# Layer 0's last pair of panels: two of its four tiles get their expert scores from TensorE, after a transpose inside the lone last panel

## The chip, the cores and the metric

The kernel runs on one core of one Trainium2 chip. The metric is the device time in microseconds of one execution; the time before is the median of three runs. A profile is one further execution, recorded instruction by instruction. Engines are named as in the profile: PE is TensorE (PEld its weight loads), DVE is VectorE, ACT is ScalarE, POOL is GpSimd, SP is the engine that issues most DMAs.

## The reference

Two layers act on 3327 nodes of 256 features. Layer 0 is

```python
x = x + relu(adj @ (layernorm(x) @ W) + b)                      # graph part
h = layernorm(x)
scores = h @ Wg.T + bg                                          # 8 experts
top2, which = top_k(scores, 2); share = softmax(top2)
x = x + sum over the two experts e of share_e * (relu(h @ W1[e].T + b1[e]) @ W2[e].T + b2[e])
```

Layer 1 has the same shape: a graph part whose adjacency is filtered by tanh(adj * adj), and a mixture of eight experts (256 by 256, gelu, two of eight per token). Everything is float32. The change concerns only `scores` of layer 0, for 256 of the 3327 tokens.

## The kernel before

**Tiling.** Nodes are padded to 3328 = 26 tiles of 128. A panel is 256 nodes (two tiles); there are 13 panels, and each has two adjacency pieces of 1.7 MB in a ring of six buffers. `x` and the support `s` stay in SBUF.

**Layer 0's graph part** is `aggregate_first` (L482). It takes panels 0 and 1 side by side, then the pairs (2,3) to (10,11) through `pair` (L571), and then panel 12 alone, the lone last panel, through `rest` (L558). `rest` runs j over the 26 tiles of source nodes; each j is two matmuls into the two PSUM banks of the panel (L495). After step `behind_` it calls `finish` (L512), and where `hooks` has an entry for j it calls that function. For the last panel the call is

```python
        rest(NPAN - 1, 0, {CJ: layer0.turn_first}, LAST_BEHIND)     # L649: CJ = 13, LAST_BEHIND = 11
```

so `finish` runs after j = 11 and works on the pair (10,11), and after j = 13 the tokens of expert block 0 are transposed (`turn_first`, L1172).

**What `finish` does for a pair.** It lists the tokens of the pair before it (`listed`), multiplies the aggregated features by the weights (`weigh`, L506) with `add_relu` on DVE (L403, L404), and then runs the generator `route0` (L1508) to its end:

1. `normalized`: statistics on DVE (L337 to L354), and for four tiles the scaling on ACT (L360), tile by tile into two `xn` buffers of two tiles each.
2. `scores` (L656): for each tile and each of eight experts one DVE product with a row of `gate` that also sums it (L662, 128x256): 32 of them for four tiles.
3. `weights` (L720): bias, ranking, the two best, `rt_both` (L700), which tells the two experts of each token.

For the earlier pairs, `pair` spreads the three steps with `next(routing)`; the last pair gets all of them in the one call.

**Listing.** `list_tokens` (L759) counts places with small matmuls on PE (`pr`, L770 and L771: from `rt_both` and the running sums `cum`), and POOL scatters each token to the lists of its two experts (`xlist`, L793). PE takes its queue in order. The last pair is listed inside expert block 0: `layer0.step(None, between=finish_last)` (L1539) runs the first product of the block (L1226), then `finish` for the lone panel, which begins with listing the pair. After that stand the transposes of block 1's tokens (L1172) and the second product of block 0 (L1323). The lone panel's own routing runs on DVE during block 1, and `plan` (L947) needs its counts.

**PSUM.** Pool `psh` (two banks) serves `ps_o` of `weigh`, `ps_h` and the turned tokens `ptb`; pool `pst` (two banks) serves `pt`, `pg`, `pr` and `pc`.

**Scores by PE** exist already in layer 1: for its lone panel, `by_features` (L377) transposes two tiles through PE and ACT copies them out (L387, L388), and `scores_by_product` (L668) multiplies them by the router `f1_r_sb` (L672), with a copy by DVE (L681). The start of the kernel loads `f1_r_sb` and four other constants through POOL's queue (L1489).

Of the kernel before, what the change touches and what calls it, by code (L numbers as in the profile page):

```python
# [10 lines left out]
F32 = mybir.dt.float32  # L11
# [11 lines left out]
P = 128  # L23
NT = 26
NP = NT * P
D = 256
DC = D // P
E = 8
H = 1024
PW = 256  # L30
NPAN = NP // PW
NCHUNK = 2
CJ = NT // NCHUNK
# [44 lines left out]
BEHIND, LAST_BEHIND = 5, 11  # L78
# [49 lines left out]
def gnn_moe_two_layers(  # L128
# [26 lines left out]
    const = ctx.enter_context(tc.tile_pool(name="const", bufs=1))  # L155
    state = ctx.enter_context(tc.tile_pool(name="state", bufs=1))
    work = ctx.enter_context(tc.tile_pool(name="work", bufs=3))
# [131 lines left out]
    def follow(later, earlier):  # L289
        for o in earlier:  # L290
            tc.add_manual_dep(later.ins, o.ins.name, after, reason="same rows of DRAM")
# [27 lines left out]
    def load_gate(g):  # L319
        nc.gpsimd.dma_start(  # L320
            out=gate.rearrange("p e d -> p (e d)"),
            in_=g.rearrange("e d -> (e d)").unsqueeze(0).partition_broadcast(P),
        )
# [53 lines left out]
    def by_features(xn, n, name="xnT"):  # L377

        return turned_tiles([xn[:, g, 0, :] for g in range(n)], name)

    def turned_tiles(tiles, name):
        n = len(tiles)
        xnT = work.tile([P, DC, n * P], F32, name=name, bufs=2)
        pt = pst.tile([P, DC, n * P], F32, name="pt", tag="pt")
        for g in range(n):
            for c in range(DC):
                nc.tensor.transpose(pt[:, c, ts(g, P)], tiles[g][:, ts(c, P)], ident)  # L387
        nc.scalar.copy(xnT, pt)  # L388
        return xnT
# [92 lines left out]
    def aggregate_first(b_sb, w, w_sb, begin, count, route, listed, freed):  # L482
# [10 lines left out]
        def add(pan, j):  # L493
            for c in range(DC):
                nc.tensor.matmul(  # L495
                    sums[pan][c],
                    lhsT=s[:, j, ts(c, P)],
                    rhs=piece(pan, j // CJ)[:, j % CJ, :],
                    start=(j == 0),
                    stop=(j == NT - 1),  # L500
                )

        def weigh(pan, g, it):
            ps = psh.tile([P, D], F32, name="ps_o", tag="ph")
            for c in range(DC):
                nc.tensor.matmul(  # L506
                    ps, lhsT=g[:, c, ts(it, P)], rhs=w_sb[:, c, :], start=(c == 0),
                    stop=(c == DC - 1),
                )
            add_relu(x[:, pan * (PW // P) + it, :], ps, b_sb)  # L510

        def finish():  # L512
            if not waiting:
                return
            todo = list(waiting)
            waiting.clear()
            if todo[0][0] < NPAN - 1:
                listed()
            for pan, g in todo:
                for it in range(PW // P):  # L520
                    weigh(pan, g, it)
            if todo[0][0] == NPAN - 1:
                listed()
            for _ in route([pan for pan, _ in todo]):
                pass

        def finishing():
# [9 lines left out]
        def sums_of():  # L537
            return work.tile([P, DC, PW], F32, name="xnT", bufs=2)

        def copy(out, ps):  # L540
            copied.append(nc.scalar.copy(out, ps))

        def count_next():
            if counts:
                count(*counts.pop(0), copied)
# [12 lines left out]
        def rest(pan, first, hooks=(), behind_=BEHIND):  # L558
            hooks = dict(hooks)
            for j in range(first, NT):  # L560
                add(pan, j)
                if j == first + behind_:
                    finish()
                if j in hooks:
                    hooks[j]()
            g = sums_of()
            for c in range(DC):
                copy(g[:, c, :], sums[pan][c])
            waiting.append((pan, g))
# [76 lines left out]
        sums[NPAN - 1] = banks[0:2]  # L646
        for _ in range(NCHUNK):
            count_next()
        rest(NPAN - 1, 0, {CJ: layer0.turn_first}, LAST_BEHIND)  # L649
        return finish  # L650

    def rows_of(a, t0, n):
        return a[t0 * P : (t0 + n) * P, :].rearrange("(n p) d -> p n d", p=P)


    def scores(xns, n, all_n=None):  # L656
        sc = work.tile([P, all_n or n, E], F32, name="rt_sc", bufs=2)
        for g in range(n):
            xn = xns[g // 2][:, g % 2, 0, 0:D]
            for e in range(E):  # L660
                product = work.tile([P, D], F32, name="rt_product", bufs=1)
                nc.vector.scalar_tensor_tensor(  # L662
                    product, xn, 1.0, gate[:, e, :], ALU.mult, ALU.mult,
                    accum_out=sc[:, g, e : e + 1],
                )
        return sc

    def scores_by_product(xnT, n, w_sb, sc=None):  # L668
        pg = pst.tile([P, n, E], F32, name="pg", tag="pt")
        for g in range(n):  # L670
            for c in range(DC):
                nc.tensor.matmul(  # L672
                    pg[:, g, :],
                    lhsT=xnT[:, c, ts(g, P)],
                    rhs=w_sb[:, c, :],
                    start=(c == 0),
                    stop=(c == DC - 1),
                )
        if sc is None:
            sc = work.tile([P, n, E], F32, name="rt_sc", bufs=2)  # L680
        nc.vector.tensor_copy(sc, pg)  # L681
        return sc
# [37 lines left out]
    def weights(sc, n, bias=None, now=False):  # L720


        if bias is not None:
            nc.vector.tensor_tensor(sc, sc, bias.unsqueeze(1).to_broadcast([P, n, E]), ALU.add)
        sel, top, both = top_two(sc, n)
        d = work.tile([P, n], F32, name="rt_d", bufs=2)
        nc.vector.tensor_tensor(d, top[:, :, 1], top[:, :, 0], ALU.subtract)
        if now:
            nc.scalar.activation(d, d, AF.Exp)
            return sel, both, shares(d, n)  # L730
        return sel, both, d
# [9 lines left out]
    def normalized(t, n, on_scalar=False):  # L741

        stats = statistics(t, n)
        if not on_scalar:
            return [layernorm(t + at, 2, stats, at) for at in range(0, n, 2)]
        shift = shifted(*stats, n)
        xns = [work.tile([P, 2, K, RW], F32, name="xn") for _ in range(0, n, 2)]
        for g in range(n):
            scaled(xns[g // 2][:, g % 2, 0, 0:D], t + g, g, stats[1], shift)
        return xns  # L750
# [726 lines left out]

    g1_wg_sb = const.tile([P, DC, D], F32, name="g1_wg_sb")
    f1_r_sb = const.tile([P, DC, E], F32, name="f1_r_sb")
    f1_b1_sb = const.tile(list(f1_b1.shape), F32, name="f1_b1_sb")  # L1480
    g1_bp_sb = const.tile(list(g1_bp.shape), F32, name="g1_bp_sb")
    for t, w in [
        (gnn_b_sb, g0_b[0:1, :].partition_broadcast(P)),
        (g1_wg_sb, g1_wg.rearrange("(c p) n -> p c n", p=P)),
        (f1_r_sb, f1_rT.rearrange("(c p) n -> p c n", p=P)),
        (f1_b1_sb, f1_b1),
        (g1_bp_sb, g1_bp),
    ]:
        follow(nc.gpsimd.dma_start(out=t, in_=w), last_normalized)  # L1489

    def count(pan, k, copied):
# [8 lines left out]
    layer0 = experts(  # L1500
        xlist0, ys0, "0", FIXED[0], H, AF.Relu, f0_w1T, f0_b1, f0_w2T, f0_b2,
        nc.scalar.copy, BLOCKS0, seven=range(3, EARLY + LATE_PAIRS + FIXED[0] - 1),
    )

    def tiles_of(pans):
        return pans[0] * (PW // P), len(pans) * (PW // P)

    def route0(pans):  # L1508
        if pans[0] == 0:
            load_gate(gates[0])  # L1510
        t, n = tiles_of(pans)
        xns = normalized(t, n, on_scalar=n == 4)
        yield
        sc = scores(xns, n)
        yield
        routed.append((xns, *weights(sc, n, f0_bg_sb), t, n, xlist0, "0"))

# [15 lines left out]
    def begin(pan):  # L1533
        if pan in (1, 8):
            fill(xlist0 if pan == 1 else xlist1)

    finish_last = aggregate_first(gnn_b_sb, g0_w, proj_sb, begin, count, route0, listed0, freed0)

    layer0.step(None, between=finish_last)  # L1539
# [192 lines left out]
    with tc.If(first_usual > 0) as arms:  # L1732
# [29 lines left out]
        with tc.If(second_usual > 0) as inner:  # L1762
# [8 lines left out]
            while len(layer1.started) < layer1.always:  # L1771
# [6 lines left out]
                with behind(last_y):  # L1778
                    if asked and asked[0][2] + 1 < at <= layer1.always - FIXED[1]:
                        yt, tiles, _ = asked.pop(0)  # L1780
                        add_loaded(yt, *tiles)
                        added.append((tiles, at))
                if waiting and at > waiting[0][1] + (1 if k < FIRST_TILES // 2 else 2):
                    tiles, _, written = waiting.pop(0)
# [4 lines left out]
                if at in (EARLY + E, EARLY + 2 * E):  # L1789
                    tiles = range(0, FIRST_TILES, 2) if at == EARLY + E else range(FIRST_TILES, MORE_TILES, 2)  # L1790
# [185 lines left out]
```

## Time and profile before

| | us |
|---|---|
| median of 3 runs (1186.8 to 1188.58) | 1188.58 |
| the profiled execution | 1192.74 |
| its span, first to last instruction | 1191.0 |
| DVE busy | 867.1 |
| products for scores, L662, x400 records | 194.9 |
| two-bank matmuls of side-by-side and lone panels, L495, x312 records | 70.2 |

A row of the profile's groups reads: line, engine, operation, output<-inputs, shapes, count, then busy time and mean duration, then the idle time of the engine just before these instructions and what ended it. The mean granted TensorE clock of the execution is 0.989 of full speed. Of 40 equal slices of the span, here is the share of PE, of DVE and the granted clock, in tenths (9 is 90% or more); the lone last panel and the first expert blocks lie in slices 10 to 12 (about 268 to 357 us):

```
PE   8999999999899999999999999999999999999973
DVE  6698999988885555454545669289999998785454
PEclk9999999999999999999999999999999999999996
```

### The profile page before, as it was taken

The numbers are of one execution on the slowest core, as the hardware profiler recorded it, in microseconds if no ns is written. First come the engines' busy times: TensorE is split into PE (matmuls) and PEld (weight loads), VectorE is DVE, ScalarE is ACT, GpSimd is POOL, SyncE is SP. The second block draws the span as 40 slices with busy tenths as digits, with TensorE's granted clock in tenths as the row PEclk, the third lists the DMA queues.
The fourth block names the chain that finished last, engine by engine and source line by source line (L and its number), as shares of the span: only waits on it lengthen the run. The fifth ranks groups of instructions, "written<-read, shape, count | busy, mean of one in ns | idle before, by whom it ended". The sixth has DMA issues, their size and how long they took to land. (4 is left out here: it accounts for less than half of the span.)

```text
span 1191.0 us, 19704 instructions
## 1 busy us (share of the span) xinstructions
PE 1152.0 (97%) x6217; PEld 1005.4 (84%) x6217; DVE 867.1 (73%) x3001; ACT 557.0 (47%) x1051; POOL 290.5 (24%) x367
## 2 busy tenths in 40 slices
PE   8999999999899999999999999999999999999973
PEld 7888888888788888888888888888888888888852
DVE  6698999988885555454545669289999998785454
ACT  5599647540233333434333346985455562043321
POOL 2111332242331112111111010022232232265531
PEclk9999999999999999999999999999999999999996
DMA  9896738724376555757565955145354451479696
GB/s 349 180 265 260 241 127 239 257 88 152 125 260 224 195 186 187 270 182 258 199 219 168 386 208 201 65 183 180 144 204 166 161 200 55 134 229 273 202 288 207
DMA packets 123185, 241.68 MB, mean 203 GB/s; under 512 B 24480, under 2 KB 93120, under 8 KB 116160
## 3 DMA queue, kind: packets, MB, share of 16 engines
q1 hardware_dynamic: 108656, 205.59, 52.7%
q0 software_dynamic: 11136, 31.60, 7.2%
q10 hardware_dynamic: 3280, 3.15, 0.8%
q8 instruction: 51, 0.84, 0.3%
q14 instruction: 62, 0.51, 0.1%
HBM read 203.98 MB, written 36.33 MB: 202 GB/s over the span
## 5 line engine op out<-in xcount | busy, mean ns | idle before, releaser
L440 PE MATMUL ps_g<-s,ring 128*128 128x256 f32 x1352 | 294.2, 380 | 0.0
L440 PEld LDWEIGHTS ps_g<-s,ring 128*128 128x128 f32 x1352 | 256.0, 190 | 34.4
L1234 ACT ACTIVATE pad<-ps_h,ring 128x256 f32<-128x256 f32 (+1 forms) x282 | 128.9, 458 | 287.2 <-PE ps_h L1226 156.1
L1226 PE MATMUL ps_h<-pad,ring 128*128 128x256 f32 (+1 forms) x1184 | 254.4, 367 | 4.4 <-ACT pad L1176 4.1
L1226 PEld LDWEIGHTS ps_h<-pad,ring 128*128 128x128 f32 x1184 | 200.9, 190 | 46.7 <-ACT pad L1234 11.1
L662 DVE SCALAR_TENSOR_TENSOR rt_product<-xn,gate 128x256 f32<-128x256 f32 x400 | 194.9, 487 | 16.1 <-ACT xn L360 2.8
L793 POOL DMA_INDIRECT ys<-pad,index x114 | 115.7, 1015 | 363.8 <-DVE pad L1281 236.1
L793 POOL DMA_INDIRECT xlist<-xn,rt_idx x104 | 115.0, 1106 | 156.9 <-DVE ln_nw L347 60.9
L1495 ACT ACTIVATE sign<-ring,below 128x416 bf16<-128x416 f32 x208 | 133.4, 641 | 13.8 <-DMA ring<-in_adjT 7.8
L470 PE MATMUL ps_g<-ring,pad 128*128 128x256 f32 x520 | 115.1, 380 | 0.8 <-DMA ring<-in_adjT 0.8
L470 PEld LDWEIGHTS ps_g<-ring,pad 128*128 128x128 f32 x520 | 98.4, 190 | 14.4 <-DMA ring<-in_adjT 1.2
L1660 ACT ACTIVATE ring<-ring 128x3328 f32<-128x3328 f32 x22 | 65.4, 2979 | 87.3 <-DVE ring L1659 56.2
L1281 DVE SCALAR_TENSOR_TENSOR pad<-ps_y,ring,pad 128x128 f32<-128x128 f32 x176 | 59.3, 348 | 47.5 <-PE ps_y L1274 47.3
L470 PE MATMUL ps_g<-ring,s 128*128 128x256 f32 x390 | 89.6, 379 | 0.0
L470 PEld LDWEIGHTS ps_g<-ring,s 128*128 128x128 f32 x390 | 74.1, 190 | 10.1
L480 DVE TENSOR_TENSOR ring<-ring,ring 128x768 f32<-128x768 f32 (+1 forms) x80 | 79.7, 1014 | 0.0
L495 PE MATMUL ps_g<-ring,s 128*128 128x256 f32 x312 | 70.2, 386 | 4.4 <-ACT s L360 4.4
L495 PEld LDWEIGHTS ps_g<-ring,s 128*128 128x128 f32 x312 | 60.1, 194 | 13.5 <-ACT s L360 5.2
L1661 ACT ACTIVATE ring<-ring 128x3328 f32<-128x3328 f32 x22 | 65.4, 2979 | 0.6
L1265 DVE TENSOR_TENSOR xnT<-pad 128x512 f32<-128x512 f32 x22 | 15.2, 692 | 59.2 <-ACT pad L1234 59.2
L1323 PE MATMUL ps_y<-ring,pad 128*128 128x256 f32 x224 | 53.8, 386 | 0.0
L776 POOL COPY xn<-rt_w 128x4 f32<-128x4 f32 x26 | 4.8, 198 | 197.8 <-DVE rt_w L738 197.8
(240 smaller groups left out, 1584.3 us busy)
## 6 DMA issues: line engine op xcount, KB each, us to landing
ring<-in_adjT SPq DMA_DIRECT2D x50, 1664.0 KB, 8.2
ring<-in_f_w1T SPq DMA_DIRECT2D x30, 1024.0 KB, 5.7
ring<-in_f_w2T SPq DMA_DIRECT2D x30, 1024.0 KB, 8.0
ring<-xlist SPq DMA_DIRECT2D x52, 258.0 KB, 3.5
ring<-in_f_w SPq DMA_DIRECT2D x36, 256.0 KB, 3.8
ring<-ys SPq DMA_DIRECT2D x12, 512.0 KB, 4.2
ring<-in_f_b SPq DMA_DIRECT2D x34, 128.0 KB, 7.6
xlist<-h2T SPq DMA_DIRECT2D x16, 257.0 KB, 7.8
```

Of the source, the lines that this page charges most:

```text
L440: nc.tensor.matmul(ps[it], lhsT=chunks[k][:, c, ts(it, P)], rhs=s[:, j, :], start=(j == 0), stop=(j == NT - 1),)
L470: nc.tensor.matmul(ps, lhsT=b[:, c, :], rhs=a[:, c, :], start=(first and c == 0), stop=(c == CJ - 1), skip_group_check=not first,)
L480: nc.vector.tensor_tensor(out[:, part, :], out[:, part, :], other[:, part, :], ALU.add)
L495: nc.tensor.matmul(sums[pan][c], lhsT=s[:, j, ts(c, P)], rhs=piece(pan, j // CJ)[:, j % CJ, :], start=(j == 0), stop=(j == NT - 1),)
L662: nc.vector.scalar_tensor_tensor(product, xn, 1.0, gate[:, e, :], ALU.mult, ALU.mult, accum_out=sc[:, g, e : e + 1],)
L793: d = nc.gpsimd.indirect_dma_start(out=a[:, :], out_offset=bass.IndirectOffsetOnAxis(ap=index, axis=0), in_=rows_, in_offset=None,)
L1226: last_product[:] = [nc.tensor.matmul(ps, lhsT=w1[:, c, ts(hc, P)], rhs=xT[:, c, :], start=(c == 0), stop=(c == DC - 1),)]
L1234: nc.scalar.activation(hT[:, hc, :], ps, func, bias=bb1[:, hc : hc + 1])
L1281: last_y[:] = [nc.vector.scalar_tensor_tensor(part, ps, xb[:, g, WT : WT + 1], part, ALU.mult, ALU.add)]
L1495: nc.scalar.activation(sign, piece(pan, k)[:, :, ts(i, GROUP)], AF.Sign, bias=below, accum_out=positive[:, pan, i, k : k + 1],)
L1660: nc.scalar.activation(a, a, AF.Square)
L1661: nc.scalar.activation(a, a, AF.Tanh)
```

## The change

The routing of the last pair is cut in three. `finish` runs only its first part (statistics and scaling), two new hooks of `rest` run the others: after j = 20, tiles 0 and 1 of the pair are transposed by PE and copied out by ACT; after j = 25, the last one, tiles 2 and 3 are scored by DVE as before (16 products), tiles 0 and 1 by four matmuls on PE with the gate weights `f0_wg_sb`, and then come the ranking and the rest. `f0_wg_sb` is one more constant, loaded at the start through POOL's queue, between `f1_r_sb` and `f1_b1_sb`. `scores` takes a range of tiles in place of an unused parameter. In the changed program the listing of the last pair and the transposes of block 1's tokens stand one after the other on PE, where they were interleaved with the first matmuls of `ps_y`; on ACT the Exp of the last pair stands after the eight `ps_h` rows of block 0, and the Exp of the lone panel before the copy of block 2's turned tokens.

```diff
@@ aggregate_first: finish
             if todo[0][0] == NPAN - 1:
                 listed()
-            for _ in route([pan for pan, _ in todo]):
+            routing = route([pan for pan, _ in todo])
+            if len(todo) == 1:
+                for _ in routing:
+                    pass
+            else:
+                next(routing)
+                last_pair.append(routing)
+
+        last_pair = []
+
+        def turn_last_pair():
+            next(last_pair[0])
+
+        def score_last_pair():
+            for _ in last_pair[0]:
                 pass
@@ aggregate_first: the lone last panel
-        rest(NPAN - 1, 0, {CJ: layer0.turn_first}, LAST_BEHIND)
+        hooks = {CJ: layer0.turn_first, CJ + 7: turn_last_pair, NT - 1: score_last_pair}
+        rest(NPAN - 1, 0, hooks, LAST_BEHIND)
@@ scores
-    def scores(xns, n, all_n=None):
-        sc = work.tile([P, all_n or n, E], F32, name="rt_sc", bufs=2)
-        for g in range(n):
+    def scores(xns, n, tiles=None):
+        sc = work.tile([P, n, E], F32, name="rt_sc", bufs=2)
+        for g in tiles or range(n):
@@ constants
     f1_r_sb = const.tile([P, DC, E], F32, name="f1_r_sb")
+    f0_wg_sb = const.tile([P, DC, E], F32, name="f0_wg_sb")
...
         (f1_r_sb, f1_rT.rearrange("(c p) n -> p c n", p=P)),
+        (f0_wg_sb, f0_wgT.rearrange("(c p) n -> p c n", p=P)),
@@ route0
         xns = normalized(t, n, on_scalar=n == 4)
         yield
-        sc = scores(xns, n)
+        if pans[-1] == NPAN - 2:
+            xnT = by_features(xns[0], 2, "h2T")
+            yield
+            sc = scores([None] + xns[1:], n, range(2, n))
+            scores_by_product(xnT, 2, f0_wg_sb, sc[:, 0:2, :])
+        else:
+            sc = scores(xns, n)
         yield
         routed.append((xns, *weights(sc, n, f0_bg_sb), t, n, xlist0, "0"))
```

## Prediction

> **What bounds the kernel now.** I read the page's busy rows first: PE is busy 97% of the span, so a change counts only by the time in which PE stands, or in which it does more or fewer matmuls. Then the waits of PE for the whole span. They sum to less than 20 us, and one of them lies at the place that the change touches:
>
> ```profile
> PE 1152.0 (97%) x6217; PEld 1005.4 (84%) x6217; DVE 867.1 (73%) x3001; ACT 557.0 (47%) x1051; POOL 290.5 (24%) x367
> ...
> PE pr L770 <- DVE rt_both L700: 3.1, 1, 3.1
> ```
>
> Next the timeline of PE around it (start, duration, line, records, idle before and releaser; one fp32 matmul of the code is two MATMUL records, a transpose is one):
>
> ```profile
> 289.44 10.53 PE L495 MATMUL ps_g<-ring,s 128*128 128x256 f32 x48
> 299.80 7.07 PE L1226 MATMUL ps_h<-pad,ring 128*128 128x256 f32 x32
> 306.71 1.89 PE L506 MATMUL ps_o<-proj_sb,xnT 128*128 128x256 f32 x8
> 311.67 0.17 PE L770 MATMUL pr<-rt_both,before 128*128 128x8 bf16 x1 [3.07 <-DVE rt_both L700]
> ...
> 311.75 1.09 PE L1172 MATMUL ptb<-ident,ring 128*128 128x128 f32 x4
> 312.64 2.60 PE L1323 MATMUL ps_y<-ring,pad 128*128 128x256 f32 x6
> ...
> 315.72 5.43 PE L1323 MATMUL ps_y<-ring,pad 128*128 128x256 f32 x24
> 320.98 7.07 PE L1226 MATMUL ps_h<-pad,ring 128*128 128x256 f32 x32
> ```
>
> The last panel ends at 299.80, block 0 of the experts begins, and at 308.60 PE stands for 3.07 us: listing the tokens of the last pair needs rt_both, the end of its scoring on DVE. The same four transposes take 0.44 us from start to next start at 327.89, but here 0.89, and the six ps_y records are 0.41 us apart, not 0.22. Windows over this stretch say why (columns: length, busy time of PE, PEld, DVE, ACT, POOL, granted clock, DMA share, GB/s):
>
> ```profile
> 308.60:311.67 3.07, 0.00 (x0) 0.00 (x0) 2.90 (x12) 0.00 (x0) 0.76 (x1) 0.98 0.34 85
> 311.67:313.00 1.33, 1.33 (x8) 1.30 (x8) 1.33 (x7) 0.12 (x1) 0.14 (x1) 0.50 0.00 0
> 313.00:314.00 1.00, 1.00 (x4) 0.75 (x3) 0.88 (x10) 0.57 (x2) 0.43 (x1) 0.50 0.00 0
> 314.00:315.00 1.00, 1.00 (x4) 0.75 (x3) 0.60 (x5) 0.00 (x0) 0.32 (x2) 0.53 0.63 86
> 315.00:316.00 1.00, 1.00 (x9) 0.78 (x8) 0.07 (x1) 0.00 (x0) 0.00 (x0) 1.00 0.34 61
> ```
>
> After the stall the clock is halved for 3.4 us. Its price: from 311.67 to block 1 at 320.98 PE takes 9.31 us; at full clock the same work is eight pr records at 0.026 (0.21), the transposes (0.44) and 32 ps_y records (6.91, from 328.33 to 335.24): 7.56. So the stall costs 3.07 + 1.75 = **4.82 us**.
>
> What DVE does meanwhile, from its timeline:
>
> ```profile
> 292.08 0.16 DVE L354 SCALAR_TENSOR_TENSOR ln_shift<-ln_mv,ln_guess 128x4 f32<-128x4 f32 x1
> 292.96 0.42 DVE L662 SCALAR_TENSOR_TENSOR rt_product<-xn,gate 128x256 f32<-128x256 f32 x1 [0.72 <-ACT xn L360]
> ...
> 311.45 0.17 DVE L700 TENSOR_SCALAR rt_both<-rt_rank 128x32 bf16<-128x32 f32 x1
> ```
>
> It is a chain without a gap: 32 products from 292.96 to 308.81 (0.47 apart; two are stretched, +0.7 together, beside a POOL copy), then 2.8 us of ranking.
>
> **The change, part by part.**
>
> *16 of 32 products go from DVE.* DVE now starts with tile 2. ACT made the four tiles from 292.33 to 294.41, 0.52 each, so tile 2 is there at 293.9 and DVE begins at 294.0 instead of 292.96. 16 x 0.47 + 0.7 ends at 302.2; a copy of the other scores out of PSUM (0.18, the row of the same copy at 1054.2), ranking 2.5 (2.8 less an add_relu op that slipped in): rt_both at **304.9**, all four cum sums by 305.7. PE, with the added work below, asks at 309.9. The stall goes, with 4.2 us to spare, and its half clock with it: -4.82.
>
> *Added to PE: four transposes and eight score records.* Layer 1's lone panel does exactly this, at full clock:
>
> ```profile
> 1051.81 0.60 PE L387 MATMUL pt<-ident,xn 128*128 128x128 f32 x4
> 1052.25 1.03 PE L1226 MATMUL ps_h<-pad,ring 128*128 128x256 f32 x4
> 1053.11 1.03 PE L672 MATMUL pg<-f_r_sb,xnT 128*128 128x8 f32 x8
> 1054.00 1.11 PE L1226 MATMUL ps_h<-pad,ring 128*128 128x256 f32 x4
> ```
>
> From start to next start: 0.44 + 0.89 = **+1.33 us**, all on the path.
>
> *Sum*: -4.82 + 1.33 = **-3.49 us**. As times: transposes 295.5 to 295.9, last panel ends at 300.24, scores to 301.13, block 0 to 308.04, ps_o to 309.93, block 1 at 317.49 instead of 320.98.
>
> *New waits.* The transposes stand in PE's queue before ten matmuls of the last panel and all of block 0. They need tiles 0 and 1 from ACT, there at 293.4: 2.1 us in hand. The score matmuls need ACT's copy out of PSUM (0.59, the row of the same shape); ACT is idle from 294.41 to 299.57, so it is done by 296.7, 3.5 us ahead. DVE's copy needs the matmuls: about 301.3, and DVE comes at 302.2. The first turn of block 1 needs a bank that add_relu of the lone panel frees: ps_o of its first tile is done at 309.1; DVE comes from rt_w, which waits for an Exp that now stands behind ACT's eighth ps_h row (308.7), so about 309.4 to 309.85; PE asks at 310.14. Thin, but 0.3 us late here costs 0.3.
>
> *ACT's order moves.* The Exp of the lone panel now stands ahead of ACT's copy of block 2's turned tokens. Block 2 needs the copy at 335.85 - 3.49 = 332.4. Before, DVE released that Exp at 331.15; with the same time the copy would end at 331.9. DVE gets to the lone panel earlier now (its rt_idx at about 312.7 instead of 316.89), so I expect the Exp near 328.
>
> *POOL and SP.* POOL's loads of proj_sb and the bias stand after the rt_w copies instead of before; nothing needs them until layer 1's features. The eight scatters of the pair start near 313.5 instead of 317.87; SP's read of block 3 at 330.08, which waited for the scatters, follows them. SP's order is unchanged, and block reads after it hang on buffers that PE frees, so they shift with PE.
>
> *One more load at the start* (f0_wg_sb, 256 short rows). The row of the same shape (f_r_sb, L1489) took POOL 0.75 us at 42.94; POOL then waited for DVE until 59.64, so the issue is hidden. It is queued behind the bias whose landing DVE awaited until 53.89; PE's next ps_o is at 59.81, so about 5 us cover it. Zero, or some tenths.
>
> *The clock rule.* The row: 3.07 us of standing brought 3.4 us of half clock; so did 2.00 us at 15.44 to 17.44 (clock 0.50 from 18.00 to 21.40). [...] I take the rows. [...]
>
> **Against which time.** The sum is made in the profiled execution: span 1191.0, 1192.74 with what lies around it; it would be 1187.5 and 1189.25. The median of the runs is 1188.58, 4.2 lower. What the stall costs isn't in proportion to the whole, so I subtract: 1188.58 - 3.49 = **1185.1**, own range 1184.2 to 1186.0.
>
> **Rivals.**
> - *The stall goes, the clock wasn't lost in the timed runs (or the transposes lose it)*: -1.74, 1186.8. [...] Against: two stalls out of two. 0.20.
> - *Hidden anyway*: a later chain keeps the end where it was, about 1188.3. For: SP's reads wait for the scatters and for buffers. Against: after 320 PE's waits for DMA are none, and the scatters come earlier. 0.07.
> - [...] 0.06.
> - *Slower*: the lone panel's Exp keeps ACT from copying block 2's tokens. The point: DVE's rt_d later than 331.4. Each us beyond stops PE for one, and from 2 us on the clock goes too (1.75). At 336 it is -3.49 + 4.6 + 1.75 = +2.9, 1191.5. For: ACT takes its queue in order. Against: even the old time of rt_d, 330.96, would do. 0.05; other mishaps 0.01.
> - The forecast: 0.60. That the routing isn't shortened is ruled out but for 0.01, since half its products leave an engine that had no gap.
>
> **Numbers.** About 0.2% (2.4 us) is what a measurement can tell from no change. Faster by more: 0.60 + 0.06 and a sliver of the first rival, 0.68; within: 0.26; slower: 0.06. The range 1183.0 to 1187.6 takes in forecast, "more" and the first rival.
>
> **What would show it.** No idle time before the listing matmuls (pr); granted clock 1.00 from 305 to 325; rt_both near 305; pg x8 starting near 300.2; block 1 at about 317.5, and from there every block 3.5 us earlier. It is wrong if PE stands before the transposes at 295.5 or before block 2 at 332.4, or if the clock still halves near 310.

## The result, and the profile after

| | before | after |
|---|---|---|
| median of 15 runs each | 1187.18 us | 1184.52 us |
| ratio, 95% interval | | 0.9978 [0.9967, 0.9988] |
| the profiled execution's span | 1191.0 us | 1184.4 us |
| its mean granted clock | 0.989 | 0.992 |

The change makes the kernel 2.7 us faster (1.4 to 3.9). The two profiled executions differ by 6.6, but 2.9 of that lies ahead of the place that changed, as will be shown.

PE's timeline at the change (start, duration, engine, line, records, and in brackets the idle time before; there is no bracket where there was none):

```profile
292.58 0.60 PE L387 MATMUL pt<-ident,xn 128*128 128x128 f32 x4
293.02 4.48 PE L495 MATMUL ps_g<-ring,s 128*128 128x256 f32 x20
297.34 0.95 PE L687 MATMUL pg<-f_wg_sb,h2T 128*128 128x8 f32 x8
298.15 7.15 PE L1241 MATMUL ps_h<-pad,ring 128*128 128x256 f32 x32
305.14 1.89 PE L506 MATMUL ps_o<-proj_sb,xnT 128*128 128x256 f32 x8
306.86 0.17 PE L785 MATMUL pr<-rt_both,before 128*128 128x8 bf16 x1
...
307.07 0.64 PE L1187 MATMUL ptb<-ident,ring 128*128 128x128 f32 x4
307.54 7.07 PE L1338 MATMUL ps_y<-ring,pad 128*128 128x256 f32 x32
314.45 7.07 PE L1241 MATMUL ps_h<-pad,ring 128*128 128x256 f32 x32
```

The stall of 3.07 us at pr is gone, and 32 ps_y records take 6.91 us from start to next start in one piece, where before they were stretched behind the stall. Windows of this execution (length, busy time of PE, PEld, DVE, ACT, POOL, granted clock, DMA share, GB/s):

```profile
305.00:310.00 5.00, 5.00 (x34) 4.37 (x33) 3.82 (x19) 1.16 (x3) 2.00 (x5) 1.00 0.23 66
310.00:315.00 5.00, 5.00 (x25) 4.41 (x24) 4.54 (x22) 0.00 (x0) 3.81 (x4) 1.00 0.30 95
```

Full clock, and PE busy throughout. DVE's timeline says by how much it is ahead now:

```profile
301.71 0.18 DVE L715 TENSOR_SCALAR rt_both<-rt_rank 128x32 bf16<-128x32 f32 x1
...
306.01 0.17 DVE L751 TENSOR_SCALAR rt_w<-rt_d 128x4 f32<-128x4 f32 x1 [3.21 <-ACT rt_d L777]
...
306.31 0.39 DVE L403 TENSOR_TENSOR gnn_t<-ps_o,gnn_b_sb 128x256 f32<-128x256 f32 x1
```

rt_both is there (301.89) 5.0 us before PE asks (306.86), and DVE, which had no gap here, now stands 3.21 us for an Exp that sits in ACT's queue behind the eighth ps_h row.

**Comparing two executions.** Absolute times can't be compared: the turns of block 0 (ptb), which come before the change acts, start at 289.00 in the one and at 286.10 in the other. In the profile before, PE stood 2.00 us for ACT (s, L360) at 15.44, and its clock was halved from 18.0 to 21.4; after, it stood 1.84 us there and the clock stayed at 1.00. So I measure stages from one PE record to another. Stage A: from the turns of block 0 to the first product of block 1 (ps_h). Stage B: from the last but one turns of layer 0 to layer 1's first features (ps_p). Here are the ends of the stages that no timeline above shows, in the first profiles of the kernel before and of the changed one:

```profile
289.00 0.60 PE L1172 MATMUL ptb<-ident,ring 128*128 128x128 f32 x4
...
665.87 0.60 PE L1172 MATMUL ptb<-ident,ring 128*128 128x128 f32 x4
...
698.42 1.99 PE L1623 MATMUL ps_p<-xnT,proj_sb 128*128 128x256 f32 x8 [0.24 <-ACT xnT L388]
```

```profile
286.10 0.60 PE L1187 MATMUL ptb<-ident,ring 128*128 128x128 f32 x4
...
659.26 0.60 PE L1187 MATMUL ptb<-ident,ring 128*128 128x128 f32 x4
...
694.22 1.99 PE L1646 MATMUL ps_p<-xnT,proj_sb 128*128 128x256 f32 x8 [0.24 <-ACT xnT L388]
```

Each ratio below is to the kernel before on the same chip. The experiments were served by three chips. On two of them every kernel takes some 1.5% longer, and PE stands 2.7 to 7.8 us within block 1 or 2; stage A ends before that.

| kernel | A, us | B, us | ratio to before, 95% interval |
|---|---|---|---|
| before (first profile) | 31.98 | 32.55 | |
| before again (e7) | 32.11 | 31.95 | 0.9996 [0.9981, 1.0011] |
| after (first profile) | 28.35 | 34.96 | 0.9978 [0.9967, 0.9988] |
| after again (e1), slower chip | 28.35 | 34.76 | 0.9971 [0.9956, 0.9986] |
| after again (e11), slower chip | 28.35 | 34.79 | 0.9977 [0.9962, 0.9992] |
| one tile by PE (e2), slower chip | 28.44 | 36.59 | 0.9965 [0.9948, 0.9982] |
| PE's work kept, all on DVE (e4) | 30.81 | 34.64 | 1.0022 [1.0005, 1.0039] |
| all four tiles by PE (e6) | 29.68 | 35.04 | 0.9992 [0.9976, 1.0008] |
| two tiles not scored at all (e8) | 27.02 | 34.82 | 0.9984 [0.9973, 0.9996] |
| listing later (e5), slower chip | 31.86 | 32.45 | 1.0031 [1.0009, 1.0052] |
| new load by SP (e3, e10), slower chips | 28.35, 28.35 | 32.76, 33.04 | 0.9977 [0.9963, 0.9991], 0.9974 [0.9960, 0.9988] |
| before and the load alone (e9), slower chip | 32.04 | 36.40 | 1.0020 [1.0004, 1.0036] |
| eight loads (e12), slower chip | 28.35 | 33.48 | 0.9969 [0.9953, 0.9985] |

Stage A repeats to 0.1 us; it shows the mechanism far better than a ratio does. Stage B, 350 us later, was in no forecast: it takes 34.64 to 36.59 us wherever POOL makes the new load once, and 31.95 to 33.48 in the other kernels. In the first two profiles the difference is 2.41. The 36.59 of e2 and the 36.40 of e9 hold 1.7 us of half clock besides, after PE stood 2.88 and 2.79 us for xnT. Between the two stages, from block 1's first product to the start of stage B, the six profiles of the fast chips agree: 344.8 to 345.2 us.

### The profile page after: what moved, and what is told of

It reads as the page before. It is cut to its first block, busy times and chain, and to the rows that moved or that the text cites. A ratio compares the mean times of both kernels' runs of the same rounds, so it can differ in the third digit from the quotient of the medians.

```text
span 1184.4 us, 19700 instructions
## 1 busy us (share of the span) xinstructions
PE 1149.5 (97%) x6229; PEld 1004.2 (85%) x6229; DVE 860.1 (73%) x2970; ACT 557.1 (47%) x1052; POOL 292.0 (25%) x368
## 5 line engine op out<-in xcount | busy, mean ns | idle before, releaser
L677 DVE SCALAR_TENSOR_TENSOR rt_product<-xn,gate 128x256 f32<-128x256 f32 x384 | 188.4, 491 | 16.3 <-ACT xn L360 3.8
```

The costliest lines, as they stand in the source:

```text
L677: nc.vector.scalar_tensor_tensor(product, xn, 1.0, gate[:, e, :], ALU.mult, ALU.mult, accum_out=sc[:, g, e : e + 1],)
```

## The experiments

**e8: the stall's worth without the price.** Two tiles get no scores of their own, but a copy of the other two's:

```diff
-            xnT = by_features(xns[0], 2, "h2T")
             yield
             sc = scores([None] + xns[1:], n, range(2, n))
-            scores_by_product(xnT, 2, f0_wg_sb, sc[:, 0:2, :])
+            nc.vector.tensor_copy(sc[:, 0:2, :], sc[:, 2:4, :])
```

> Left out: the scores of two of the four tiles; the scores of the other two are copied in their place, so 256 tokens go to other experts. Nothing is added to PE. Theory: the stall and its half clock gone without the price, 4.8 us faster than before and 1.33 us faster than the changed kernel up to block 2. Rival (the stall's half clock comes back elsewhere, or PE's added work was hidden in other waits): block 2 no earlier than in the changed kernel.

Stage A is 27.02: 4.96 us less than before (4.82 forecast), and 1.33 less than the change, to the hundredth. The added matmuls were hidden in no wait. The ratio, 0.9984, falls short of 4.8 us: it is 1.9 (0.5 to 3.2), and stage B gives back 2.3.

**e6: twice the work on PE.**

```diff
-            xnT = by_features(xns[0], 2, "h2T")
+            xnT = [by_features(q, 2, name) for q, name in zip(xns, ("h2T", "xnT"))]
...
-            sc = scores([None] + xns[1:], n, range(2, n))
-            scores_by_product(xnT, 2, f0_wg_sb, sc[:, 0:2, :])
+            sc = work.tile([P, n, E], F32, name="rt_sc", bufs=2)
+            for i in range(2):
+                scores_by_product(xnT[i], 2, f0_wg_sb, sc[:, 2 * i : 2 * i + 2, :])
```

> All four tiles of the pair by PE: 8 transposes, 16 score records, no product on DVE. Theory (once the stall is gone, work on PE is a pure price): 1.33 us slower than the changed kernel, 2.2 us faster than before. Rival (more is better, since DVE's chain still holds something else up): as fast as the changed kernel or faster.

Stage A: 29.68, which is 1.33 more than with two tiles. e8, the change and e6 lie on one line: each two tiles on PE cost 1.33 us, and once the stall is gone nothing is bought by more of it.

**e4: PE's work kept, the products back on DVE.**

```diff
-            sc = scores([None] + xns[1:], n, range(2, n))
-            scores_by_product(xnT, 2, f0_wg_sb, sc[:, 0:2, :])
+            sc = scores(xns, n)
+            unused = pst.tile([P, 2, E], F32, name="pg", tag="pt")
+            for g in range(2):
+                for c in range(DC):
+                    nc.tensor.matmul(unused[:, g, :], lhsT=xnT[:, c, ts(g, P)], rhs=f0_wg_sb[:, c, :], ...)
```

> PE keeps the added work (4 transposes, 8 score records, whose results nothing reads), but DVE scores all four tiles again. Theory (it is DVE's shorter chain that pays): PE stands for what is left of the stall, 3.07 - 1.33 = 1.74 us, at the listing. If a gap of 1.7 us still halves the clock, the next turns of block 1 are where the kernel before has them (total: as before, or up to 0.3 us later); if it doesn't, 1.75 us earlier. In both cases 1.7 to 3.5 us slower than the changed kernel. Rival (the new place of the listing or of the scatters pays, not DVE): as fast as the changed kernel.

PE's timeline, and a window, of e4:

```profile
310.98 0.18 PE L785 MATMUL pr<-rt_both,before 128*128 128x8 bf16 x1 [1.50 <-DVE rt_both L715]
...
311.70 0.66 PE L1187 MATMUL ptb<-ident,ring 128*128 128x128 f32 x4 [0.33 <-DVE gnn_t L403]
```

```profile
312.00:314.00 2.00, 2.00 (x15) 1.63 (x14) 2.00 (x14) 0.77 (x2) 0.89 (x3) 1.00 0.19 66
```

The stall is back, cut to 1.50 us by the work that fills it, and stage A is 2.46 us longer than with the change. So the gain comes from DVE's shorter chain, not from the new places of the listing and the scatters. The clock stays at 1.00: a gap of this length didn't cost the half clock. In all, e4 should be about 1.2 us slower than before (1.2 won in stage A, 2.4 lost in B); it is 2.6 (0.6 to 4.6). The bracket of ptb is new: the turns wait for DVE too, for the PSUM bank that its add (gnn_t) frees.

**e5: another cure for the same stall.** From the kernel before, the listing goes behind block 0's last product; no work moves to PE:

```diff
-            if todo[0][0] == NPAN - 1:
-                listed()
...
     layer0.step(None, between=finish_last)
+    with tc.issue_after(last_product[0].ins):
+        list_tokens(*routed.pop(0))
     layer0.step(None)
```

> The kernel before with another cure for the same stall: no work moves to PE, DVE scores all four tiles, but the listing of the last pair stands behind block 0's last product in PE's queue instead of before it. Theory (stall 3.07 plus half clock 1.75, cured without added PE work): 4.8 us faster than the kernel before, 1.3 us faster than the changed kernel; no idle time at pr, granted clock 1.00 from 305 to 325. Rival (block 0's last product is too late for the scatters and the reads behind them, or the products can't begin because their own operands wait): PE stands at block 2 or 3 instead, and the time is that of the kernel before or worse.

```profile
304.37 1.89 PE L506 MATMUL ps_o<-proj_sb,xnT 128*128 128x256 f32 x8
309.24 0.66 PE L1170 MATMUL ptb<-ident,ring 128*128 128x128 f32 x4 [2.98 <-DVE gnn_t L403]
309.73 8.76 PE L1321 MATMUL ps_y<-ring,pad 128*128 128x256 f32 x32
```

My theory fell here. The wait moved by one instruction and kept its size: DVE reaches the lone panel's add behind the whole ranking of the pair, and only the add frees the bank that the turns need. ps_y takes 8.76 us instead of 7.07, since the clock halves again (0.61 and 0.53 in the windows 310 to 314). Stage A is 31.86, as before. The scatters start 42.3 us behind the turns of block 0 instead of 28.9, and in block 2 PE then stands for another 7.8 us, where the other kernels on such a chip stand 2.7 or 2.8. The stall in the profile carried the name of the listing, but what was late was DVE, and it held PE by two handles.

**e2: is one tile enough?**

```diff
-            xnT = by_features(xns[0], 2, "h2T")
+            xnT = turned_tiles([xns[0][:, 0, 0, :]], "h2T")
...
-            sc = scores([None] + xns[1:], n, range(2, n))
-            scores_by_product(xnT, 2, f0_wg_sb, sc[:, 0:2, :])
+            sc = scores(xns, n, range(1, n))
+            scores_by_product(xnT, 1, f0_wg_sb, sc[:, 0:1, :])
```

> Only one tile of the pair is transposed and scored by PE, DVE keeps 24 of 32 products. Theory (the gain is the stall and the half clock after it; what PE adds is a pure price): rt_both is ready about 308.3 on the before kernel's axis, 1 us ahead of PE's question at 309.3, so the stall stays away and only 0.67 us of work is added: 0.67 us faster than the changed kernel, 4.15 us faster than the kernel before. Rival (one tile isn't enough): rt_both comes after 309.3, PE stands again for what is missing, the clock may halve again, and the time is 0 to 2 us above the changed kernel.

```profile
306.61 0.17 PE L785 MATMUL pr<-rt_both,before 128*128 128x8 bf16 x1
...
307.55 0.66 PE L1187 MATMUL ptb<-ident,ring 128*128 128x128 f32 x4 [0.60 <-DVE gnn_t L403]
```

For the listing it is enough, with 1.0 us in hand (rt_both starts at 305.44 and ends at 305.62). For the bank it isn't: 0.67 us less work on PE, 0.60 us of waiting for the add. Stage A is 28.44, the same as with two tiles.

**e1, e7, e11: the same kernels again.**

> The changed kernel once more, unaltered: a second profile and more timed runs. Theory (the 1.8 us given back at the end of layer 0 were chance of the first profiled execution): time 0.2 to 0.3% below the kernel before, no idle time before the listing matmuls (pr), and the loads of the expert outputs (s<-ys) of layer 0's end issued 11.5 us behind block turns at about 634, as before the change, not 13.3. Rival (the change causes it): 13.3 again, and PE again waits at the first-weights load of a late expert block.

> The kernel before, unaltered, for a profile from a chip on which the changed one was profiled too. Theory: PE stands about 3 us at the listing (pr) for rt_both and has half clock for 3.4 us after it, also here; against a profile of the changed kernel from the same chip, the change is worth 3.5 us between the first turns (ptb) and block 2's. Where block 1's products stood 3.5 us for ACT while the scatters ran in the runs of the changed kernel, this kernel shows such waits too, one block later, since its scatters run 8 us later. Rival (the earlier scatters of the change make these waits): none here, and the gain is smaller than 3.5 us on such a chip.

> The changed kernel, unaltered, as the other side of that comparison. Theory: 35.3 us from the first turns to block 2's if the chip does not stand in block 1, 34.6 to 35 us at the end of layer 0, and by these two sums 1.1 us faster than the kernel before. Rival (the give-back is not there in timed runs): 2.7 to 3.5 us faster, as the first two comparisons had it.

Stage A repeats (28.35 three times; 31.98 and 32.11). Stage B's 34.8 was no chance either: in e1 the loads of the expert outputs are issued 13.35 us behind the turns again, as its rival had it. Of the slower chips, e7 shows nothing, as it ran on a fast one; e9 below, which has the order of the kernel before, stands within block 1 too, for 2.7 us in two gaps. So the earlier scatters of the change don't make these waits.

**e3 and e10: the new load on SP's queue.** One line moves, so that POOL issues the DMAs that it issued before:

```diff
+            nc.sync.dma_start(out=f0_wg_sb, in_=f0_wgT.rearrange("(c p) n -> p c n", p=P))
...
-        (f0_wg_sb, f0_wgT.rearrange("(c p) n -> p c n", p=P)),
```

> The changed kernel, with the new weights' load moved from POOL's queue to SP's, so that POOL issues exactly the DMAs that it issued before the change. Theory (chance): same time as the changed kernel within 0.1%, and the end of layer 0 varies from one execution to another in both. Rival (the additional POOL load shifts by one which earlier transfers POOL's later ones wait for, and so delays the puts of layer 0's last block): the 1.8 us come back here, 1.8 us faster than the changed kernel, s<-ys loads 11.5 us after the last block's turns instead of 13.3.

> The changed kernel with the new load on SP's queue, again, to be compared on one chip with the changed kernel itself. Theory: 32 to 32.8 us from the third late block's turns to the features, where the changed kernel has 34.6 to 35; 3.5 us faster than the kernel before and 2.3 us faster than the changed kernel. Rival (what is won there is lost again behind it, as the two medians of the first comparison suggest, 0.5 us apart): no difference from the changed kernel.

Stage B is 32.76 and 33.04, as without the change. POOL's puts of expert outputs near it, first in the kernel before (e7), then in the changed one:

```profile
646.50 0.97 POOL L793 DMA_INDIRECT ys<-pad,index  x1 [11.24 <-DVE pad L1281]
647.77 1.48 POOL L793 DMA_INDIRECT ys<-pad,index  x1 [0.30 <-ACT pad L1234]
```

```profile
640.94 0.96 POOL L808 DMA_INDIRECT ys<-pad,index  x1 [11.23 <-DVE pad L1296]
644.60 0.97 POOL L808 DMA_INDIRECT ys<-pad,index  x1 [2.70 <-DVE pl_v L917]
```

SP's loads of these outputs, in the same two profiles:

```profile
650.96 1.48 SPq L1405 DMA_DIRECT2D s<-ys  x3
```

```profile
647.18 1.49 SPq L1420 DMA_DIRECT2D s<-ys  x3
```

The second put follows the first by 1.27 us in the one and by 3.66 in the other. The loads come later too: counted from the first put, they are issued after 4.46 us in the kernel before and after 6.24 in the changed one. The loads of the next weights queue behind them, and PE finds them missing in the changed kernel:

```profile
663.55 7.23 PE L1241 MATMUL ps_h<-pad,ring 128*128 128x256 f32 x32 [1.53 <-DMA ring<-in_f_w1T]
```

In e3 and e10 the puts are 1.28 and 1.27 us apart again.

**e9: the load alone.** The kernel before, with nothing but the tile f0_wg_sb and its load on POOL's queue.

> The kernel before with one part of the change alone: the load of f0_wg_sb on POOL's queue; nothing reads it, DVE still scores all four tiles. Theory (this load causes what is given back at the end of layer 0, since it moves every later DMA of POOL on by one in the rotation of completion semaphores): stall and half clock at the listing as in the kernel before, 38.9 us from the first turns to block 2's, and from the turns of the third late block to layer 1's features 34.6 to 35 us instead of 32 to 32.6; in all 2.4 us slower than the kernel before. Rival (the give-back comes with the scores by PE or the earlier scatters): 32 to 32.6 us there, and the time of the kernel before.

```profile
653.39 0.97 POOL L793 DMA_INDIRECT ys<-pad,index  x1 [11.24 <-DVE pad L1281]
657.06 0.97 POOL L793 DMA_INDIRECT ys<-pad,index  x1 [2.70 <-DVE pl_v L902]
```

The puts are 3.67 us apart, stage B is 36.40, and the kernel is 2.4 us slower (0.5 to 4.3). Neither PE's scores nor the earlier scatters are in it: an 8 KB load at 41.5 us, which nobody waits for, delays a put 615 us later.

**e12: seven loads more.** The compiled kernel gives POOL's DMAs eight completion semaphores in turn: in all 14 profiles the 228 to 236 DMAs of POOL take the numbers 111 to 118 one after the other, without an exception. If the place in this rotation is what matters, eight more DMAs are as good as none:

```diff
+    more = [const.tile([P, DC, E], F32, name=f"more{i}") for i in range(7)]
...
+        *[(m, f0_wgT.rearrange("(c p) n -> p c n", p=P)) for m in more],
```

> The changed kernel with seven further loads of the same weights on POOL's queue, into tiles that nothing reads, so that POOL issues eight more DMAs than before the change. Theory (what counts is the place in a rotation over eight completion semaphores): each later DMA has the semaphore that it had before the change, and the end of layer 0 takes 32 to 32.8 us again; POOL's 5 us more at the start are hidden behind its wait for DVE. Rival (a DMA more on POOL costs by itself): 35 us or more there.

The puts are 1.27 us apart and stage B is 33.48: the delay isn't the price of a load, and the place in the rotation fits. It doesn't explain all. In the kernel before, the next pair of puts is the one that is spread, 4.56 us (660.03 and 664.59 in e7, likewise in e3, e5 and e10); with one load more that pair stands 1.27 apart (654.48 and 655.75), so the spread has moved to the pair before; and in e12, with the places of the kernel before, neither pair is spread. POOL's timeline of e12 shows the rotation at work:

```profile
40.68 0.64 POOL L320 DMA_DIRECT2D gate<-gate  x1 [33.64 <-DMA gate<-in_f_wgT]
...
43.99 2.15 POOL L1508 DMA_DIRECT2D more<-in_f_wgT  x3
53.24 0.71 POOL L1508 DMA_DIRECT2D more<-in_f_wgT  x1 [7.11 <-DMA gate<-gate]
```

The ninth load stands 7.1 us until the first of these nine has landed. Why just the put at 644.60 waits when it is one place on isn't settled, so the rotation is argued, while the load as the cause is shown (e9, e3, e10). The releaser that the profile names (DVE's clearing of pl_v, a table of the plan) is no input of the put; it lies just ahead of a branch on POOL that follows this put in the program.

**What stays open.** The repaired versions (e3, e10, e12) save 1.3 to 2 us in stage B of their profiles, but beside the changed kernel on the same chip their medians are lower by 0.46, 0.18 and 0.64 us only. Either the runs without a profile give back less there, or the 2 us are lost again later. In the profiles they aren't lost: from ps_p to the end the repaired versions take 495.4 to 498.7 us, the changed kernel on the same chips 500.3 and 500.7. But these are single executions; e9's interval reaches down to 0.5 us, so the first is possible. A part of what the timed runs have over the stages lies in the clock: on the two slower chips their mean granted clock is 0.9885 with the change (e1, e11) and 0.9855 and 0.9858 before, two stretches of 3.41 us at half clock (0.0014 each), where the stall accounts for one. Where the other lies isn't known. A version that measurably beats the change wasn't found.

## Why the prediction was right, by its own steps

- **The stall and its half clock, -4.82.** -4.96 in e8. Both parts were real, and both came from DVE, as e4 shows.
- **PE's added work, +1.33.** 1.33 in e8 and in e6. The row of layer 1's lone panel gave it exactly.
- **The sum, -3.49.** Stage A fell by 3.63 between the first profiles. With the 2.90 us added that the changed kernel is ahead at the turns of block 0, block 1 starts at 317.35 on the old axis (forecast 317.49), pg at 300.24 (300.24) and rt_both at 304.61, done at 304.79 (304.9). From there every block was to come 3.5 us earlier; this held up to stage B (344.88 and 344.81 us between the stages), and not behind it.
- **"Thin, but 0.3 us late here costs 0.3": the bank for the turns.** The right place, too lightly taken. It held in the change, where DVE frees it 0.37 us ahead of the turns' question; one tile less, and it cost 0.60; in e5 it was the whole stall.
- **"ACT's order moves".** The lone panel's Exp ran at 324.02 and ACT's copy for block 2 at 324.13, 4.6 us before PE needed it. On the old axis that is 326.9, where the forecast had the Exp near 328. The rival built on it didn't come.
- **"Zero, or some tenths": the one more load at the start. This step failed.** I looked only at what could wait for the load near 43 us. It did hide there; but it moved every later DMA of POOL by one semaphore, and stage B, from 659 us on, is 2.4 us longer in the first profiles. That the forecast of the time held all the same is in part luck, as the last step says.
- **The clock.** I took the rows. Rightly: 4.96 us can't be had from a stall of 3.07 alone. But "two stalls out of two" was a wrong reading, and "from 2 us on" with it: the same profile has one of 2.45 us at 5.79 and one of 2.57 us at 1133.20, and the clock stayed at 1.00 behind both (the last section lists them). The first rival, that the timed runs kept their clock (-3.07 + 1.33 = -1.74), fails on average: the mean granted clock of 59 runs of the kernel before is 0.9906, and on the same chip 0.9918 in e8 and 0.9924 in e6, where one stretch of 3.41 us at half clock is worth 0.0014 (half of 3.41 in 1188 us). Whether a single timed run kept it isn't shown. The added transposes were no threat: four of them take 0.44 us, and the changed kernel's clock is 1.00 in the window 292.00 to 297.30; behind the eight of e6 (0.87 us) 20 ps_g records take 4.32 us, as behind the four. No run shows the gain that "more" stands for: the changed kernel's clock is halved near the end too, 0.50 from 1154.39 to 1157.80 (before: from 1161.46 to 1164.88).
- **The time.** Forecast 1185.1, measured 1184.52. That these two are so close is in part luck. The forecast subtracted 3.49 from a median of three runs, 1188.58; fifteen runs gave 1187.18 for the same kernel, and the gain measured against them is 2.7 (1.4 to 3.9), and 3.5 and 2.8 in the two repeats. The cost of stage B wasn't in the sum; by the first profiles, stage A less stage B, the gain should be 1.2 us. That the runs show more is the open point above.

## What to carry to other kernels

Ask of a stall which engine is late, not which instruction carries it: here two waits hung on one DVE chain, and moving the named one changed nothing. Count an added DMA also by where it moves all later ones of its queue: here a load that nobody waits for cost about 2.4 us some 600 us later, and another queue avoided it. Measure between two records near the change, since stage A repeated to 0.1 us where medians of 13 to 22 runs leave more than 1 us open.

## What the runs showed of the hardware

**The granted clock behind a stall of PE.** These are all stalls of PE of 1.8 us or more ahead of its last matmul, in the first profiles of the two kernels:

| kernel | stall from, us | its length, us | granted clock behind it |
|---|---|---|---|
| before | 5.79 | 2.45 | 1.00 |
| before | 15.44 | 2.00 | 0.50 from 17.98 to 21.39 |
| before | 308.60 | 3.07 | 0.50 from 311.55 to 314.96 |
| before | 1133.20 | 2.57 | 1.00 |
| before | 1157.18 | 3.08 | 0.50 from 1161.46 to 1164.88 |
| after | 5.69 | 2.56 | 1.00 |
| after | 15.42 | 1.84 | 1.00 |
| after | 1151.51 | 2.33 | 0.50 from 1154.39 to 1157.80 |

So the length of a stall alone doesn't tell whether the clock halves: 2.57 us left it, 2.00 us halved it. Another 2.00 us, in e10 from 15.63, left the 64 ps_g records behind it at 0.22 us each (14.08 us in all). The stalls of 2.98 (e5), 3.04 (e9), 3.07 and 3.11 us (e7) at the listing or the turns were all followed by half clock: 0.53 from 312 to 314 in e5, 0.50 from 311 to 313 in e9, and in e7 six ps_y records 0.39 us apart instead of 0.22. The 1.50 us of e4 were not: its clock is 1.00 from 309 to 325.

**Slower chips.** On two of three chips PE stands within block 1 (40 to 42 us from the turns of block 0 to those of block 2 in the changed kernel, 35.3 on a fast chip), while POOL's scatters run. The profile names no releaser for PE's wait; in e1 ACT's row at 321.50, which PE goes on from at 322.03, begins 1.2 us after PE's last product (320.31). What differs between these chips isn't known.
